# Position terms of the attention keys: added by VectorE, or by accumulating transfers onto keys that ScalarE copies

## The chip, the cores and the metric

The kernel runs on one core of one Trainium2 chip. The core has five engines with a queue each: TensorE (PE, with its weight loads PEld), VectorE (DVE), ScalarE (ACT), GpSimd (POOL) and SyncE (SP, which here only issues transfers). They work at the same time and wait for each other through semaphores. Sixteen DMA engines move data between DRAM and the on-chip memory SBUF; matrix products land in a second on-chip memory, PSUM. The metric is the device time of one execution in microseconds (us); less is better.

## What is computed

Eight images of 512 channels x 32 x 32 pass through two blocks. The change lies in the first block, in an attention over the 1024 pixels of an image. Cut to it, with `cbs` for convolution, normalization and silu:

```python
def bot_attention(x, qkv_w, rw, rh):
    b, c, h, w = x.shape
    hw = h * w
    qkv = conv2d(x, qkv_w, 0).reshape(b, 3, HEADS, HD, hw)
    q, k, v = (qkv[:, 0], qkv[:, 1], qkv[:, 2])
    r = (rw + rh).reshape(1, HEADS, HD, hw)
    logits = jnp.einsum('bhdi,bhdj->bhij', q, k + r) * HD ** (-0.5)
    a = jax.nn.softmax(logits, axis=-1)
    out = jnp.einsum('bhij,bhdj->bhdi', a, v)
    return out.reshape(b, c, h, w)
...
t = cbs(x, cv1_w, cv1_bn, 0)
ys = [t[:, :C], t[:, C:]]
for i in range(N):
    yi = ys[-1]
    z = cbs(yi, m_cv1_w[i], m_cv1_bn[i], 1)
    z = bot_attention(z, m_qkv_w[i], m_rw[i], m_rh[i])
    z = jax.nn.silu(bn_eval(conv2d(z, m_cv2_w[i], 0), m_cv2_bn[i]))
    ys.append(yi + z)
return cbs(jnp.concatenate(ys, axis=1), cv2_w, cv2_bn, 0)
```

There are 4 heads of 64 channels (so 256 channels, two halves of 128 partitions), N = 2 layers, and all is fp32. What matters is `k + r`: the position terms `r` are the same for every image. The second block (a depthwise 3x3 convolution of nine taps per channel, then a 1x1 convolution, both with a pruning of channels) is computed between the parts of the next image's attention.

## The kernel before

An image is a tile of [128 partitions, 4 chunks, 1024 pixels]. For each image, and each of the two layers, the stages are: the 3x3 convolution by a Winograd-like transform (`conv3`: products into `ps_c3`), queries, keys and values (`qkv`), attention (`attention`), a 1x1 convolution with residual (`cv2m`); then the convolution over the four parts (`last_conv` or `quartered`) and the second block.

The order of work is written out by hand. Each stage registers its pieces under a short name with `add(...)`, and strings of names (`FIRST`, `HEAD`, `TAIL`, `LAST`) say in which order the pieces are issued; `go` walks such a string. Image 0 follows `FIRST`; images 1 to 7 follow `HEAD`, then `TAIL` or, for the last, `LAST`. The wrapper `InOrder` keeps the issue order on each of PE, DVE, ACT and SP, so a name that is moved in a string moves its instruction in the queue of its engine. All of these instructions carry line 105 in the profile, that of the wrapper; POOL's carry their own lines (the prune `lp` is line 615).

The names that the change and the prediction speak of:

- `k`: four pieces of matmuls that make the keys, half 0 and half 1 (k m=2 and 3 in the code), into a PSUM tile `ps_qk` of [128, 2, 512]. Such tiles come from `ps_big`, which has two buffers and is shared with the values `ps_v`, the queries and the scores `ps_s`: a new tile waits until an old one is emptied.
- `kd`: one transfer by SP that loads `r` for both halves (1 MB) from DRAM (`r_dram`, written once in image 0 by `positions`) into the tile `kr`.
- `ka`: two additions by VectorE, `kr[:, m] = ps_qk + kr[:, m]`, which also empty the PSUM tile.
- `v`, `va`: values and their copy to SBUF by ScalarE (`vt`). `q`, `qa`: the same for queries (`qy`).
- `s`, `e`, `p`, `w`: for each of 32 steps of a layer, scores on PE from `kr` and `qy` (16 steps on half 0, then 16 on half 1), exponentials on ScalarE, their sums on VectorE, products with the values on PE.
- `t`, `l`, `lr`, `lp`: taps of the depthwise convolution (VectorE), its relu and range (ScalarE), its prune (GpSimd). `X` loads the exponential's table on ScalarE.

`kr`, `vt` and `qy` also serve as scratch of `conv3` before. In image 0 the keys take another path (`columns`, `lines`), since `r` isn't in DRAM yet.

Of the kernel before, what the change touches and what calls it, by code (L numbers as in the profile page):

```python
# [12 lines left out]
ALU = mybir.AluOpType  # L13
AX = mybir.AxisListType

P = 128
B, C, F = 8, 512, 32
# [45 lines left out]

HEAD = """
    t c*2 t b im id bm c ca iv t ip t l t*2 ib lr b t*3 c bm ca b y d y bm d ya d*2 ya d*3 y P d
    Rc R d*2 P Rc R d P ya d kd Rc R B P Rc R P B*2 Rc R E P Ez Rc B R E Ez y k*3 ya k ka t X lp
    ka t*4 v*2 l t va v*2 va t lr q*2 t*2 lp t q qa s e q qa s e p s t e w t p s e w l p s*2 w
    e*2 p w s p e s w t s w t s e*2 p lr e p w*2 h z s e p w s t w s p s e p e*2 w p s w p e w s
    t e p s w s e w e t p*2 w lp t h z s*2 e p e w s*2 n e*2 w p w s nr s p e w nr e p s e w nr
    s nr t p ns l w e p*2 w lr lp w ot h s e s w p ot s w ot s e*2 p*2 e w p s w e w s e p*2 z  # L70
    sc w nc w*2 h n nc o O nr ok Ok sc z nr*3 ns o ou oa O*2 Ou sc m Oa m sc nc m ma m ma mr ma
    ot mr ma mr o nc mr d ou Ou o O d ou Ou o d O ou*2 oa Ou*2 d Oa o O P d*2 Rc d*3 R P kd d*2
    Rc R d P Rc P R B Rc P B Rc P R B*2 Rc R ou E oa Ou R Oa o O dp E Ez*2 X k v*2 k ou oa Ou
    fr*2 Oa ka fr f*2 fr f*2 dx va k v*2 va k q*2 ka q qa q qa s e s*2 e p e w p s e p w s*2 e*2
    p*2 w s*2 e*2 w*2 s g p e w*2 s e w p s*2 h g e g p w s w z p e*2 s w e g*2 s*2 w*2 p e*2 g
    p*3 g s w*2 e p s e w h s*2 e*2 p z p w*2 s p e p s n w nr*3 w e s g e p w p s e p w*2 s nc
    e nr s ns e nc w s h s p w z w e p s e w s p e*2 p sc s w e p*2 w s sc e p w*3 h n nr*4 ns z
"""

TAIL = """  # L80
# [45 lines left out]
def fast_kernel(  # L126
# [16 lines left out]
    nc = Engines(tc)  # L143
# [12 lines left out]
    def const_tile(shape, name):  # L156
        return const.tile(shape, F32, tag=name, name=name)
# [4 lines left out]
    def big_tile(name):  # L162
        return ps_big.tile([P, 2, 512], F32, tag="big", name=name)
# [33 lines left out]
    z = const_tile([P, 2, HW], "z")  # L197

    qy = const_tile([P, 2, HW], "qy")
    kr = const_tile([P, 2, HW], "kr")  # L200
# [38 lines left out]
    r_dram = [dram.tile([P, 2, HW], F32, tag=f"r{l}", name="r") for l in range(2)]  # L239
# [15 lines left out]
    sc = const_tile([P, NBN], "sc")  # L255
# [29 lines left out]
    def flat(ps):  # L285
        return ps.rearrange("p n f -> p (n f)")
# [5 lines left out]
    def phases(ap):  # L292

        return ap.rearrange("p (r h t) -> p r h t", h=F, t=F // 4)
# [12 lines left out]
    def add(name, *pieces):  # L307
        todo.setdefault(name, []).extend(pieces)
# [104 lines left out]
    def ring_load(n=1):  # L413
        for _ in range(n):
            if not sources:
                continue
            if holds and len(sources) <= holds[0]:
                waiting[0] += 1
                continue
            src = sources.pop(0)  # L420
            t = ringp.tile([P, 2048], F32, tag="ring", name="wring")
            o = t[:, : src[1]]
            if src[1] == 1024:
                o = o.rearrange("p (k o) -> p k o", o=P)
            nc.sync.dma_start(o, src[0])
            ring.append(t)
# [463 lines left out]
    def qkv(l, by_input):  # L890


        wt, tiles, values = [], {}, {}

        def weights():
            if not wt:
                wt.append(ring.pop(0)[:, : 6 * C2].rearrange("p (k o) -> p k o", k=2))
            return wt[0]

        def products(m, k):  # L900
            w = weights()
            if m not in tiles:
                tiles[m] = big_tile("ps_qk")
            for n in range(2):
                nc.tensor.matmul(
                    tiles[m][:, n, :],
                    w[:, k, m * P : (m + 1) * P],
                    z[:, k, n * 512 : (n + 1) * 512],
                    start=(k == 0),
                    stop=(k == 1),  # L910
                )

        full = [P, 4, F, F // 4]

        def load_positions():
            nc.sync.dma_start(kr, r_dram[l])

        def add_positions(m):
            nc.vector.tensor_tensor(kr[:, m, :], flat(tiles.pop(m + 2)), kr[:, m, :], ALU.add)


        def columns(m):
            col = rw[:, l, m, :].rearrange("p (t r) -> p r t", r=4)
            nc.vector.tensor_tensor(
                phases(kr[:, m, :]),
                phases(flat(tiles.pop(m + 2))),
                col.unsqueeze(2).to_broadcast(full),
                ALU.add,
            )

        def lines(m):
            row = rh[:, l, m, :].unsqueeze(1).unsqueeze(3)
            kk = phases(kr[:, m, :])
            nc.gpsimd.tensor_tensor(kk, kk, row.to_broadcast(full), ALU.add)

        def value_products(g, js):
            w = weights()
            if g not in values:
                values[g] = ps_big.tile([P, 4, C2], F32, tag="big", name="ps_v")
            for j in js:  # L940
                jt = 4 * g + j
                for k in range(2):
                    nc.tensor.matmul(
                        values[g][:, j, :],
                        z[:, k, jt * P : (jt + 1) * P],
                        w[:, k, 2 * C2 : 3 * C2],
                        start=(k == 0),
                        stop=(k == 1),
                    )

        def value_end(g):
            nc.scalar.copy(vt[:, 4 * g : 4 * g + 4, :], values.pop(g))

        def query_end(m):
            nc.scalar.copy(qy[:, m, :], flat(tiles.pop(m)))

        order = [(k, m) for m in (2, 3) for k in range(2)]
        add("k", *[lambda m=m, k=k: products(m, k) for k, m in (sorted(order) if by_input else order)])
        if by_input:
            add("ka", *[lambda m=m: columns(m) for m in range(2)])  # L960
            add("kp", *[lambda m=m: lines(m) for m in range(2)])
        else:
            add("kd", load_positions)
            add("ka", *[lambda m=m: add_positions(m) for m in range(2)])
        add("v", *[lambda g=g, j=j: value_products(g, (j, j + 1)) for g in range(2) for j in (0, 2)])
        add("va", *[lambda g=g: value_end(g) for g in range(2)])
        add("q", *[lambda m=m, k=k: products(m, k) for m in range(2) for k in range(2)])
        todo["q"].append(lambda last=todo["q"].pop(): (last(), ring_load()))
        add("qa", *[lambda m=m: query_end(m) for m in range(2)])
# [402 lines left out]
    for b in range(B):  # L1372
# [26 lines left out]
        for l in range(2):  # L1399
            conv3(l)  # L1400
            qkv(l, first)
            attention()
            cv2m(l)
# [471 lines left out]
```

## Time and profile before

| What | Value |
|---|---|
| Runs | median 2597.78 us of 4 (2596.92 to 2601.54) |
| The profiled execution | 2596.29 us, of which the span on the core is 2594.5 us |
| Granted TensorE clock | 0.998 |
| kr<-ps_qk,kr on DVE | 28 of 1.225 us (median) |
| vt<-ps_v on ACT (a copy of the same shape from PSUM) | 32 of 1.01 us (median) |
| kr<-r issued by SP | 14 of 1 MB, 7.1 us to landing (median) |
| r<-pos issued by SP | 4 of 512 KB, 3.4 us to landing (median) |
| pt<-in_x issued by SP | 32 of 512 KB, 3.9 to 11.8 us to landing (median 9.7) |
| ht<-ht,keep on POOL (the prune) | 28 of 1.12 to 2.12 us |

The span is the time from the first to the last instruction on the core. In the lines that follow, "A <- B" behind a duration says that the engine stood idle before A until B was done. A matmul of fp32 is recorded as two, and the end of a matmul is modelled, so records of neighbours overlap a little; gaps under 0.16 us between matmuls can hide in that. Times in the timeline are counted from the start of the span.

### The profile page before, as it was taken

Reading aid. Unit: us, or ns where it says so; the run is one execution under the profiler, and the core shown is the slowest. Engines: PE = TensorE matmul, PEld = TensorE weight load, DVE = VectorE, ACT = ScalarE, POOL = GpSimd, SP = SyncE. Lnnn points to the kernel's source line nnn. Section 1 sums busy time; section 2 is a strip of 40 time slices with the busy share of each in tenths; the row PEclk is TensorE's granted clock in tenths of the full one; section 3 lists DMA queues with packets and bytes.
Section 4 is the critical chain, followed back from the end, with each engine's and each line's share of the span. In section 5 each row is a group of like instructions: output and inputs, shape, how many; then the busy total and the mean of one; then the engine's idle time right before and its main releaser. Section 6 shows DMA issues by size and latency. Waiting matters only on the chain.

```text
span 2594.5 us, 36342 instructions
## 1 busy us (share of the span) xinstructions
PE 2558.0 (99%) x14806; PEld 1291.6 (50%) x14806; DVE 2084.9 (80%) x2982; ACT 1185.8 (46%) x1523; POOL 98.0 (4%) x71
## 2 busy tenths in 40 slices
PE   8999999999999999999999999999999999999997
PEld 5454463634636346463464635545355554645443
DVE  8887589877898878887788778887788877888657
ACT  3635436353462544635445344444445444353534
POOL 1000000000000000000000000000000000000000
PEclk9999999999999999999999999999999999999999
DMA  9445230522305113060130602206121151312300
GB/s 345 158 156 202 66 122 25 188 77 73 113 27 212 53 65 122 17 248 17 65 123 17 248 17 81 107 18 246 33 98 74 60 204 33 137 36 95 112 17 34
DMA packets 81773, 268.49 MB, mean 103 GB/s; under 512 B 6848, under 2 KB 37312, under 8 KB 65600
## 3 DMA queue, kind: packets, MB, share of 16 engines
q1 hardware_dynamic: 78048, 262.69, 28.5%
q10 hardware_dynamic: 3552, 3.41, 0.4%
q8 instruction: 118, 1.93, 0.3%
q14 instruction: 55, 0.45, 0.1%
HBM read 212.34 MB, written 36.96 MB: 96 GB/s over the span
## 4 chain that ended last, share of the span: by engine, by line
PE 93%; DVE 3%; ACT 2%; DMA 1%; issue 0%; ACTq 0%; POOL 0%; SPq 0%; DVEq 0%
PE ps_av L105 17%; PE ps_s L105 16%; PE ps_c L105 13%; PE ps_cv L105 11%; PE ps_qk L105 8%; PE ps_cv2q L105 8%; PE ps_q L105 6%; PE ps_v L105 4%; PE ps_m L105 4%; PE ps_y L105 4%; PE ps_dn L105 2%; ACT qy L105 1%; DVE ht L105 1%; PE ps_pw L105 0%; DVE sum L105 0%
## 5 line engine op out<-in xcount | busy, mean ns | idle before, releaser
L105 ACT ACTIVATE e<-ps_s 128x1024 f32<-128x1024 f32 x512 | 509.7, 1023 | 287.5 <-PE ps_s L105 266.1
L105 PE MATMUL ps_s<-qy,kr 64*64 64x512 f32 x4096 | 514.6, 592 | 1.5
L105 DVE TENSOR_TENSOR sum<-sum,e 128x1024 f32<-128x1024 f32 x384 | 475.6, 1238 | 40.2 <-ACT e L105 21.0
L105 PE MATMUL ps_av<-e,vt 64*64 64x512 f32 x4096 | 507.0, 590 | 0.0
L105 DVE SCALAR_TENSOR_TENSOR ht<-xn,v_sb,ht 128x961 f32<-128x961 f32 (+1 forms) x256 | 312.3, 1228 | 8.3 <-ACT ht L105 5.0
L105 PEld LDWEIGHTS ps_s<-qy,kr 64*64 64x64 f32 x4096 | 160.8, 132 | 288.8 <-issue 183.7
L105 PEld LDWEIGHTS ps_av<-e,vt 64*64 64x64 f32 x4096 | 165.9, 133 | 277.0 <-issue 266.5
L105 PE MATMUL ps_qk<-z,wring 128*128 128x512 f32 x512 | 229.8, 596 | 2.0 <-ACT z L105 1.3
L105 DVE TENSOR_TENSOR sum<-e 128x1024 f32<-128x1024 f32 x64 | 78.2, 1221 | 126.1 <-ACT e L105 124.8
L105 ACT COPY c<-ps_c 128x256 f32<-128x256 f32 x96 | 35.6, 371 | 262.3 <-PE ps_c L105 262.3
L105 PEld LDWEIGHTS ps_qk<-z,wring 128*128 128x128 f32 x512 | 95.7, 190 | 118.5 <-issue 100.0
L105 DVE RECIPROCAL r<-ps_dn 128x128 f32<-128x128 f32 x128 | 112.8, 923 | 11.3 <-PE ps_dn L105 9.0
L105 PEld LDWEIGHTS ps_c<-kr,wring 128*128 128x128 f32 x1024 | 116.8, 192 | 8.0 <-issue 7.7
L105 PE MATMUL ps_c<-vt,wring 128*128 128x128 f32 x1024 | 118.2, 276 | 2.1 <-DMA wring<-u 1.4
L105 PE MATMUL ps_c<-qy,wring 128*128 128x128 f32 x1024 | 117.3, 275 | 0.5 <-ACT c L105 0.5
L105 PEld LDWEIGHTS ps_c<-vt,wring 128*128 128x128 f32 x1024 | 116.2, 192 | 3.0 <-ACT c L105 2.4
L105 PE MATMUL ps_c<-kr,wring 128*128 128x128 f32 x1024 | 117.0, 275 | 0.0
L105 PE MATMUL ps_cv<-pt,w_sb 128*128 128x512 f32 x256 | 116.7, 607 | 0.0
L105 PEld LDWEIGHTS ps_c<-qy,wring 128*128 128x128 f32 x1024 | 115.7, 192 | 0.7 <-ACT c L105 0.7
L105 PE MATMUL ps_v<-wring,z 128*128 128x256 f32 x512 | 114.8, 379 | 0.7 <-DVE kr L105 0.7
L105 PE MATMUL ps_m<-z,wm_sb 128*128 128x512 f32 x256 | 112.5, 592 | 0.0
L105 PE MATMUL ps_y<-pt,w_sb 128*128 128x512 f32 x256 | 112.3, 592 | 0.0
(177 smaller groups left out, 3233.2 us busy)
## 6 DMA issues: line engine op xcount, KB each, us to landing
wring<-u SPq DMA_DIRECT2D x96, 1024.0 KB, 4.9
pt<-in_x SPq DMA_DIRECT2D x32, 512.0 KB, 9.7
rw<-r SPq DMA_DIRECT2D x64, 256.0 KB, 3.4
xt<-in_x SPq DMA_DIRECT2D x32, 512.0 KB, 5.9
out<-xt SPq DMA_DIRECT2D x32, 512.0 KB, 3.3
kr<-r SPq DMA_DIRECT2D x14, 1024.0 KB, 7.1
wring<-q SPq DMA_DIRECT2D x14, 896.0 KB, 5.7
wring<-in_wqkv SPq DMA_DIRECT2D x16, 768.0 KB, 4.6
```

What stands on the lines that cost most here:

```text
L105: made = method(*args, **kwargs)
```

## The change

Keys are copied from PSUM to `kr` by ScalarE (`ka` is now that copy), and the position terms are added to them by one transfer of GpSimd for each half that accumulates from DRAM into `kr` (`kd`, now behind `ka`). The load of `r` by SP is gone. The string `HEAD` has the new names in their places and some others moved; it has two names more than before. The descriptor scratch that the program sets aside is given a size of 2048 bytes per partition, where before nothing was said of it.

```diff
-        def load_positions():
-            nc.sync.dma_start(kr, r_dram[l])
+        def keys(m):
+            nc.scalar.copy(kr[:, m, :], flat(tiles.pop(m + 2)))
 
         def add_positions(m):
-            nc.vector.tensor_tensor(kr[:, m, :], flat(tiles.pop(m + 2)), kr[:, m, :], ALU.add)
+            nc.gpsimd.dma_start(kr[:, m, :], r_dram[l][:, m], accum_op=ALU.add)
...
-            add("kd", load_positions)
-            add("ka", *[lambda m=m: add_positions(m) for m in range(2)])
+            add("ka", *[lambda m=m: keys(m) for m in range(2)])
+            add("kd", *[lambda m=m: add_positions(m) for m in range(2)])
...
-    nc = bacc.Bacc("TRN2", target_bir_lowering=False, num_devices=1)
+    nc = bacc.Bacc("TRN2", target_bir_lowering=False, num_devices=1, dynamic_dma_scratch_size=2048)
```

In `HEAD`, around the keys of the first and of the second layer:

```diff
-    Rc R d*2 P Rc R d P ya d kd Rc R B P Rc R P B*2 Rc R E P Ez Rc B R E Ez y k*3 ya k ka t X lp
-    ka t*4 v*2 l t va v*2 va t lr q*2 t*2 lp t q qa s e q qa s e p s t e w t p s e w l p s*2 w
+    Rc R d*2 P Rc R d ya P d Rc R B P Rc R P B*2 Rc R E P Ez Rc B R E Ez y k*3 ya k ka X lp ka
+    kd*2 t*5 v*2 l t va v*2 va t lr q*2 t*2 lp t q qa s q e qa s e p s t e w t s e w l s*2 p*2 w
...
-    ot mr ma mr o nc mr d ou Ou o O d ou Ou o d O ou*2 oa Ou*2 d Oa o O P d*2 Rc d*3 R P kd d*2
+    mr ot mr ma mr o nc mr ou d Ou o O d ou Ou o d O ou*2 oa Ou*2 d Oa o O P d*2 Rc d*3 R P d*2
...
-    Rc R d P Rc P R B Rc P B Rc P R B*2 Rc R ou E oa Ou R Oa o O dp E Ez*2 X k v*2 k ou oa Ou
-    fr*2 Oa ka fr f*2 fr f*2 dx va k v*2 va k q*2 ka q qa q qa s e s*2 e p e w p s e p w s*2 e*2
+    Rc R d P Rc P R B Rc P B Rc P R B*2 Rc R ou E oa Ou R Oa o O dp E Ez*2 X k v k v ou oa Ou
+    fr*2 Oa ka kd f*2 fr*2 f*2 dx va k v*2 k va q*4 ka kd qa*2 s*3 e*2 p e w p s e w s*2 e*2 p*3
```

The rest of `HEAD` has further moves by a place or a few of sums, products and checks (`p`, `w`, `ot`, `sc`, `m`, `fr`, `g`).

More of the change, by code (lines that the diff above doesn't have):

```diff
@@ L65 @@
     t c*2 t b im id bm c ca iv t ip t l t*2 ib lr b t*3 c bm ca b y d y bm d ya d*2 ya d*3 y P d
-    Rc R d*2 P Rc R d P ya d kd Rc R B P Rc R P B*2 Rc R E P Ez Rc B R E Ez y k*3 ya k ka t X lp
-    ka t*4 v*2 l t va v*2 va t lr q*2 t*2 lp t q qa s e q qa s e p s t e w t p s e w l p s*2 w
-    e*2 p w s p e s w t s w t s e*2 p lr e p w*2 h z s e p w s t w s p s e p e*2 w p s w p e w s
-    t e p s w s e w e t p*2 w lp t h z s*2 e p e w s*2 n e*2 w p w s nr s p e w nr e p s e w nr
-    s nr t p ns l w e p*2 w lr lp w ot h s e s w p ot s w ot s e*2 p*2 e w p s w e w s e p*2 z
@@ L71 @@
-    sc w nc w*2 h n nc o O nr ok Ok sc z nr*3 ns o ou oa O*2 Ou sc m Oa m sc nc m ma m ma mr ma
-    ot mr ma mr o nc mr d ou Ou o O d ou Ou o d O ou*2 oa Ou*2 d Oa o O P d*2 Rc d*3 R P kd d*2
-    Rc R d P Rc P R B Rc P B Rc P R B*2 Rc R ou E oa Ou R Oa o O dp E Ez*2 X k v*2 k ou oa Ou
-    fr*2 Oa ka fr f*2 fr f*2 dx va k v*2 va k q*2 ka q qa q qa s e s*2 e p e w p s e p w s*2 e*2
-    p*2 w s*2 e*2 w*2 s g p e w*2 s e w p s*2 h g e g p w s w z p e*2 s w e g*2 s*2 w*2 p e*2 g
-    p*3 g s w*2 e p s e w h s*2 e*2 p z p w*2 s p e p s n w nr*3 w e s g e p w p s e p w*2 s nc
@@ L77 @@
-    e nr s ns e nc w s h s p w z w e p s e w s p e*2 p sc s w e p*2 w s sc e p w*3 h n nr*4 ns z
+    Rc R d*2 P Rc R d ya P d Rc R B P Rc R P B*2 Rc R E P Ez Rc B R E Ez y k*3 ya k ka X lp ka
+    kd*2 t*5 v*2 l t va v*2 va t lr q*2 t*2 lp t q qa s q e qa s e p s t e w t s e w l s*2 p*2 w
+    e*2 p w s p e s w t s w t e s e p lr e p w*2 h z s e p w s t w s p s e p e*2 w*2 p s e w s t
+    e p s w p s e w e t p*2 w lp t h z s*2 e*2 w s*2 n e p*2 e w*2 s nr s p e w nr e p s e w nr
+    s nr t p ns l w e p*2 w lr lp w ot h s e s w p ot w s w s e*2 p*2 e w p s e w s e ot p*2 z
@@ new lines @@
+    sc w nc w*2 h n nc o O nr ok Ok z nr*2 sc nr ns o ou oa O*2 Ou sc Oa m sc nc m*2 ma*2 m ma
+    mr ot mr ma mr o nc mr ou d Ou o O d ou Ou o d O ou*2 oa Ou*2 d Oa o O P d*2 Rc d*3 R P d*2
+    Rc R d P Rc P R B Rc P B Rc P R B*2 Rc R ou E oa Ou R Oa o O dp E Ez*2 X k v k v ou oa Ou
+    fr*2 Oa ka kd f*2 fr*2 f*2 dx va k v*2 k va q*4 ka kd qa*2 s*3 e*2 p e w p s e w s*2 e*2 p*3
+    w s*2 g e*2 w*2 s p e w*2 s e w p s*2 h g e g p w s w z p e*2 s w e g*2 s*2 w*2 p e*2 g p*3
+    g s w*2 e p s e w h s*2 e*2 p z p w*2 s p e p s n nr*3 w e s g e p w p s w*3 e p s nc e nr s
@@ L78 @@
+    ns e nc w s h s p w z w e p s e w s p e*2 p sc s w e p*2 w s sc e p w*3 h n nr*4 ns z
 """
```

## The prediction

> **What bounds the kernel now.** I read the page first (busy time by engine, then the chain that ended last), then TensorE's own waits for everything after the first image, then the timelines of the two stages in which keys are made, and last the windows of DMA load around them.
>
> The page's engine shares and its chain of waits:
>
> ```profile
> PE 2558.0 (99%) x14806; PEld 1291.6 (50%) x14806; DVE 2084.9 (80%) x2982; ACT 1185.8 (46%) x1523; POOL 98.0 (4%) x71
> PE 93%; DVE 3%; ACT 2%; DMA 1%; issue 0%; ACTq 0%; POOL 0%; SPq 0%; DVEq 0%
> ```
>
> TensorE (PE) carries 93% of the chain and VectorE (DVE) 3%. A busy PE need not be a full one, so I ask how regular it is. The windows of whole stretches of 315 us (columns: us, then busy us and count of PE, PEld, DVE, ACT, POOL, then clock, DMA share, GB/s):
>
> ```profile
> 955.00:1270.00 315.00, 314.75 (x1842) 159.36 (x1841) 256.48 (x369) 143.97 (x188) 10.71 (x7) 1.00 0.27 97
> 1270.00:1585.00 315.00, 314.75 (x1842) 159.16 (x1842) 256.87 (x369) 144.00 (x187) 10.70 (x7) 1.00 0.27 97
> ```
>
> PE idles 0.25 us in 315. All that PE waited for from 320 us to the end:
>
> ```profile
> PE ps_pw L105 <- DVE wring L105: 4.7, 1, 4.7
> PE pv L105 <- DVE d L105: 1.7, 2, 0.8
> PE ps_c L105 <- ACT c L105: 0.5, 1, 0.5
> PE pv L105 <- DVE flag L105: 0.4, 1, 0.4
> PE pk L105 <- DVE gm L105: 0.3, 1, 0.3
> ```
>
> That is 7.6 us in all, and none of it names kr. The waits on kr (0.7 us) lie before 320 us, in the first image, which takes another path (`columns`/`lines`). The changed path runs 7 images x 2 layers = 14 times.
>
> Now the stage of layer 0 in the second image (start, duration, engine, what, count; a fp32 matmul is recorded as two):
>
> ```profile
> 372.30 7.03 PE L105 MATMUL ps_qk<-z,wring 128*128 128x512 f32 x16
> 375.93 1.23 DVE L105 TENSOR_TENSOR kr<-ps_qk,kr 128x1024 f32<-128x1024 f32 x1 [3.89 <-PE ps_qk L105]
> 379.16 7.07 PE L105 MATMUL ps_v<-wring,z 128*128 128x256 f32 x32
> 379.36 1.23 DVE L105 TENSOR_TENSOR kr<-ps_qk,kr 128x1024 f32<-128x1024 f32 x1 [1.02 <-PE ps_qk L105]
> 391.31 1.09 PE L105 MATMUL ps_s<-qy,kr 64*64 64x512 f32 x8
> ```
>
> The keys of half 0 are out of PSUM at 377.2, and the first score that reads them starts at 391.3: PE fills the gap with values and queries. Layer 1, the same image:
>
> ```profile
> 510.14 3.60 PE L105 MATMUL ps_qk<-z,wring 128*128 128x512 f32 x8
> 512.06 1.22 DVE L105 TENSOR_TENSOR kr<-ps_qk,kr 128x1024 f32<-128x1024 f32 x1 [0.93 <-PE ps_qk L105]
> 513.57 3.62 PE L105 MATMUL ps_v<-wring,z 128*128 128x256 f32 x16
> 525.70 3.32 PE L105 MATMUL ps_s<-qy,kr 64*64 64x512 f32 x24
> ```
>
> And the load on the DMA engines in these two stages (the share is the last column but one):
>
> ```profile
> 379.00:383.00 4.00, 4.00 (x19) 3.40 (x18) 3.60 (x4) 0.00 (x0) 0.65 (x1) 1.00 0.02 4
> 383.00:387.00 4.00, 4.00 (x18) 3.13 (x18) 3.89 (x5) 2.87 (x3) 0.00 (x0) 1.00 0.00 0
> 504.00:530.00 26.00, 25.92 (x103) 13.39 (x105) 15.29 (x19) 11.86 (x13) 0.00 (x0) 1.00 0.94 356
> ```
>
> Layer 0 has idle DMA engines, layer 1 nearly full ones: there the loads of pt and xt and the stores of out pass.
>
> **What the Trainium skill says.** "DMA: Bandwidth & Descriptors", section "SWDGE vs HWDGE vs iDMA": an accumulating transfer has to be issued by GpSimd, whose cores write its descriptors in software; the same page's "Anatomy of one DMA — SWDGE (gpsimd) path" prices a plain one at about 2.0 us plus bytes / 436e3, here 2.0 + 524,288 / 436e3 = 3.2 us, and "Latency and other measured facts" puts its first byte at about 1 us. The trace of before has no transfer from GpSimd; its plain 512 KB transfers from SP take 3.4 us (r<-pos, median) on free engines and 11.8 us at worst (pt<-in_x) in the crowd of layer 1. "SBUF — State Buffer", section "Who interferes with whom": GpSimd and VectorE share a port pair, and an instruction of one with two SBUF inputs holds up one of the other that reads SBUF. The trace agrees: the prune on POOL takes 1.12 us in the best case and 2.12 us beside taps with two SBUF inputs. It infers that descriptor writing is not held by such VectorE work, only by its two-port modes. No page prices the accumulation itself.
>
> **The change part by part.**
>
> *VectorE loses the addition.* 28 TENSOR_TENSOR kr<-ps_qk,kr of 1.225 us = 34.3 us less, so 2084.9 becomes about 2050.6. It is worth nothing to the end: in the steady images PE idles 0.25 us.
>
> *ScalarE gains a copy.* 28 copies of 128x1024 from PSUM; the same form is there as vt<-ps_v, 1.01 us. 28 x 1.01 = 28.3 us, 1185.8 becomes about 1214. In layer 0 the first stands behind y<-ps_y, which ends at 373.98, and before the table load; it runs when its matmuls end, 375.93 to 376.94. The load and the 0.20 us warm-up follow until 378.4; the second copy starts at 379.4, undelayed, and ends at 380.4. So PSUM is freed 0.2 us earlier than now, and the values that take these buffers (379.2 and 382.6) don't wait. Behind them in ScalarE's queue stand ht (waits for taps that VectorE now does about 4 us earlier, since it no longer waits for ps_qk) and vt, which still finds its matmuls ended at 382.6.
>
> In layer 1 PE's order becomes k v k v for k v v k in pieces of 1.72 us: the first key half ends at 510.1 rather than 511.9, the copy at 511.2, before PE wants the buffer at 511.8. va ends at 512.9, the values that reuse its buffer start at 513.5: 0.6 us to spare. The second key half moves to 517.0–518.7, its copy after va on ScalarE to 519.8; the second query tile needs that buffer at 522.1. Nothing stalls. The other swaps move single scores or values in PE's queue. Counted in the order of both programs, a score stays at least 2 pieces behind the score whose PSUM buffer it takes (as before) and a value 3 pieces behind its score (as before), at 0.86 us a piece against 1.02 us of exponential. Cost: 0.
>
> *SP loses the loads of kr* (14 issues, of 1 MB). In layer 1 this takes 1 MB out of the full stretch before 500 us; the ring loads behind it come earlier. Worth 0: no wait of PE after 320 us is on a DMA.
>
> *GpSimd gains 28 issues.* In layer 0 the prune stands ahead of them; its keep is computed once VectorE is through with y, near 372.2, so even 2.12 us of it ends by 374.4, before the copy. Behind the two issues stands the next prune, at 390.7 now, whose result is needed some 60 us later.
>
> *The new wait.* PE's first score of a layer waits for the accumulation of half 0, with all of attention behind it in PE's queue. Room from the end of the copy: layer 0 391.31 − 376.94 = 14.4 us; layer 1 525.70 − 511.2 = 14.5 us. Half 1 is read by the 17th score, near 418.6 in the timeline of layer 0: 38 us of room. Bounds of the time from copy to landing: below, 1 + 3.2 = 4.2 us by the page. Above, the accumulation also reads its destination: I double the trace's times, 1 + 2 x 3.4 = 7.8 us in layer 0 and 1 + 2 x 11.8 = 24.6 us in layer 1. The worst pt stands last of four in one queue behind other loads; GpSimd's has a queue of its own (so the first section named; the engines alternate between queues), so I take 8 us for layer 0 and 10 us for layer 1. Both are inside the room: cost 0.
>
> *The smaller scratch* sets how many descriptors can be outstanding. Two transfers at a time and over 100 us between pairs: I take 0. If it held up the second of a pair, that one has 38 us.
>
> Sum: 0 on PE. The profiled execution took 2596.3 us (span 2594.5 and 1.8 around it); the median of the runs is 2597.8, 1.5 us above it, and that is what I forecast. Its own range, from the spread of the runs shown and small shifts of the end, is 2594 to 2602.
>
> **Rivals.** About 0.2%, 5.2 us, is what a measurement of this kernel can tell from no change.
>
> *Late landing in layer 1 (slower).* From 14.5 us between copy and landing on, each further us costs 7 us. At 16 us: 7 x 1.5 = 10.5, so 2608; at the upper bound of 24.6 us: 7 x 10.1 = 71, so 2669. For it: the share of 0.94, the untried accumulation. Against it: its own queue and 1 MB less ahead.
>
> *GpSimd is held up by VectorE in layer 0 (slower).* The taps run back to back there until 391.8. If descriptors were written only in the gaps after that, the landing would be at about 391.8 + 4.2 = 396: 4.7 us late, 7 x 4.7 = 33, so 2631. For it: the doubled prune. Against it: the page's inference, and that writing is not reading.
>
> *VectorE's relief reaches PE (faster).* At most the 7.6 us of waits after 320 us, so 2590. Of these 4.7 us lie at the end of the last image, where the chain is VectorE's work on the last convolution, which doesn't begin earlier; against it, then, the regular 0.25 us.
>
> **How the numbers follow.** Hidden on both layers 0.66; late landing 0.19; held-up descriptors 0.08; relief 0.07. That gives within 0.2% 0.66, slower 0.27, faster 0.07. The range runs from 2592.5, the edge of no change, to 2614, which takes in late landings up to 2.3 us at one layer; left out are 0.07 below and some 0.13 above.
>
> **What would show it.** ACT near 1214 and DVE near 2051 us; a new queue of about 15 MB or its double; no wait of ps_s on kr among PE's waits; the steady windows still at 314.75 of 315. A wait of PE ps_s on the DMA kr<-r, seven or fourteen times, would prove the forecast wrong, and its length the landing time; a wait of ps_v or ps_qk on ACT kr would show the 0.6 us margin mistaken.

## The result, and the profile after

| Kernel | Median | Range | Runs |
|---|---|---|---|
| before | 2598.06 us | 2596.57 to 2601.54 | 52 |
| changed | 2595.51 us | 2593.91 to 2596.44 | 32 |

The ratio is 0.9989, its 95% interval 0.9985 to 0.9994: 2.55 us faster (1.6 to 3.9 by the interval). That is little, inside the 0.2% that the forecast set as its bound, but it is not nothing: the interval leaves 1 out, and no change had been forecast. The profiled execution of before (2596.29 us) lies below all 52 runs of before, so the two profiles, 2594.5 and 2593.9 us of span, show only part of the difference; e4_before, below, finds out why.

The page of the changed kernel (engine shares; the queues with packets, MB and share of the 16 engines; one row of the DMA issues):

```profile
PE 2557.1 (99%) x14806; PEld 1291.6 (50%) x14806; DVE 2054.8 (79%) x2954; ACT 1213.9 (47%) x1551; POOL 130.2 (5%) x99
...
q1 hardware_dynamic: 76032, 248.01, 27.2%
q0 software_dynamic: 4032, 14.68, 3.1%
...
kr<-r POOLq DMA_DIRECT2D x28, 512.0 KB, 6.6
```

VectorE has lost 30 us and ScalarE gained 28. A new queue carries 14.68 MB, counted once. All that TensorE waited for from 320 us on:

```profile
PE ps_pw L105 <- DVE wring L105: 4.7, 1, 4.7
PE pv L105 <- DVE d L105: 1.7, 2, 0.8
PE pv L105 <- DVE flag L105: 0.5, 1, 0.5
PE pk L105 <- DVE gm L105: 0.2, 1, 0.2
```

There is no wait on kr, and one line of before is gone, PE ps_c <- ACT c. Windows of the same two stretches read as before; they cannot show the gain, because a stretch of fixed length is full of records either way:

```profile
955.00:1270.00 315.00, 314.79 (x1842) 159.50 (x1841) 252.56 (x366) 148.22 (x192) 15.16 (x11) 1.00 0.29 97
1270.00:1585.00 315.00, 314.78 (x1841) 159.38 (x1840) 251.41 (x364) 147.77 (x192) 16.25 (x11) 1.00 0.29 97
```

The timeline of layer 0 in the second image, keys to first score:

```profile
376.58 1.01 ACT L105 COPY kr<-ps_qk 128x1024 f32<-128x1024 f32 x1 [1.95 <-PE ps_qk L105]
...
378.17 1.05 POOL L919 DMA_DIRECT2D kr<-r  x1 [3.30 <-ACT kr L105]
...
381.55 0.87 POOL L919 DMA_DIRECT2D kr<-r  x1 [2.33 <-issue]
...
391.96 1.09 PE L105 MATMUL ps_s<-qy,kr 64*64 64x512 f32 x8
```

From the ps_qk of this layer (372.95) to the first score it takes 19.01 us, as before (391.31 − 372.30). Layer 1:

```profile
510.77 1.01 ACT L105 COPY kr<-ps_qk 128x1024 f32<-128x1024 f32 x1 [1.29 <-PE ps_qk L105]
...
512.08 0.89 POOL L919 DMA_DIRECT2D kr<-r  x1 [70.42 <-ACT kr L105]
...
512.50 1.01 ACT L105 COPY vt<-ps_v 128x1024 f32<-128x1024 f32 x1 [0.71 <-PE ps_v L105]
...
514.01 3.62 PE L105 MATMUL ps_v<-wring,z 128*128 128x256 f32 x16
...
526.14 2.26 PE L105 MATMUL ps_s<-qy,kr 64*64 64x512 f32 x16
```

From the ps_qk of layer 1 to its first score it takes 20.83 us in both (505.31 to 526.14, and 504.87 to 525.70 before). The stages in which keys are made cost what they cost before. So the gain lies elsewhere. Aligning the starts of TensorE's work in both traces, one place differs in nearly every image: the sums of the exponentials at the end of layer 0's attention. VectorE collects them in the tile `sum`, and TensorE adds them over the partitions by a product with ones, into `ps_dn`. Its weight load for the second half of ps_dn waits there for VectorE's sum. Two images of before, then two of after (start, duration; in brackets the wait of the weight load):

```profile
1400.75 0.14 PEld L105 LDWEIGHTS ps_dn<-sum,ones 128*32 128x32 f32 x4 [0.69 <-DVE sum L105]
1717.19 0.14 PEld L105 LDWEIGHTS ps_dn<-sum,ones 128*32 128x32 f32 x4 [0.69 <-DVE sum L105]
```

```profile
1716.60 0.14 PEld L105 LDWEIGHTS ps_dn<-sum,ones 128*32 128x32 f32 x4 [0.50 <-DVE sum L105]
2032.83 0.14 PEld L105 LDWEIGHTS ps_dn<-sum,ones 128*32 128x32 f32 x4 [0.50 <-DVE sum L105]
```

The image takes 316.44 us before and 316.23 after. The wait is 0.69 or 0.70 us in all seven images of before, and 0.49 or 0.50 in six of the changed kernel. In its fifth image it is 0.85 us. VectorE was some 0.2 us late there already, and then GpSimd's prune takes 3.11 us and VectorE stands idle for it inside the chain that ends in the sum:

```profile
1388.55 3.11 POOL L615 TENSOR_SCALAR ht<-ht,keep 128x1024 f32<-128x1024 f32 x1 [12.76 <-DVE keep L105]
...
1391.70 1.23 DVE L105 TENSOR_TENSOR pt<-ht,pt 128x1024 f32<-128x1024 f32 x1 [0.94 <-POOL ht L615]
```

In the next image the same prune takes 2.02 us, and VectorE doesn't wait for it. TensorE's own row hides the wait for the sum, since the eight matmuls are merely recorded as a longer group. Before:

```profile
1399.92 1.89 PE L105 MATMUL ps_dn<-sum,ones 128*32 128x512 f32 x8
```

After:

```profile
1715.96 1.69 PE L105 MATMUL ps_dn<-sum,ones 128*32 128x512 f32 x8
```

### The profile page after: what moved, and what is told of

Same layout as the page of the kernel before. It is cut to its first block, busy times and chain, and to the rows that moved or that the text cites. A ratio compares the mean times of both kernels' runs of the same rounds, so it can differ in the third digit from the quotient of the medians.

```text
span 2593.9 us, 36377 instructions
## 1 busy us (share of the span) xinstructions
PE 2557.1 (99%) x14806; PEld 1291.6 (50%) x14806; DVE 2054.8 (79%) x2954; ACT 1213.9 (47%) x1551; POOL 130.2 (5%) x99
## 3 DMA queue, kind: packets, MB, share of 16 engines
q1 hardware_dynamic: 76032, 248.01, 27.2%
q0 software_dynamic: 4032, 14.68, 3.1%
## 4 chain that ended last, share of the span: by engine, by line
PE 94%; DVE 3%; ACT 1%; issue 1%; DMA 0%; ACTq 0%; POOL 0%; SPq 0%; DVEq 0%
PE ps_av L105 16%; PE ps_s L105 16%; PE ps_c L105 13%; PE ps_cv L105 11%; PE ps_qk L105 8%; PE ps_cv2q L105 8%; PE ps_q L105 7%; PE ps_v L105 4%; PE ps_m L105 4%; PE ps_y L105 4%; PE ps_dn L105 1%; ACT qy L105 1%; DVE sum L105 1%; DVE ht L105 1%; PE ps_pw L105 0%
## 5 line engine op out<-in xcount | busy, mean ns | idle before, releaser
L105 DVE SCALAR_TENSOR_TENSOR ht<-xn,v_sb,ht 128x961 f32<-128x961 f32 (+1 forms) x256 | 317.5, 1248 | 8.6 <-ACT ht L105 5.0
```

What stands on the lines that cost most here:

```text
L105: made = method(*args, **kwargs)
```

## The experiments

Each was run beside the kernel before; the medians of before were 2597.98 to 2598.75 us. The changed kernel's 2595.51 us is from its own runs above. Most ratios lie within 0.5% of 1, so an interval that holds 1 settles nothing by time; there the traces are compared. The theories of where the gain comes from: ORDER (other moves in HEAD), RELIEF (VectorE's time saved reaches TensorE), SCRATCH (the smaller descriptor scratch), CHANCE (the scatter of the runs), and, formed after the first four runs, TAIL (the order of VectorE's sums at the end of layer 0's attention) and SP-LOAD (the load that SP no longer issues).

### Order and keys apart

e1_order: the order of the changed kernel with the keys of before.

```diff
-    Rc R d*2 P Rc R d P ya d kd Rc R B ...
+    Rc R d*2 P Rc R d ya P d kd Rc R B ...
...
-    ... Ez*2 X k v*2 k ou oa Ou
+    ... Ez*2 X k v k v ou oa Ou
```

> The arithmetic of the kernel before (SP loads the position terms, VectorE adds them, kd and ka at their old places among their neighbours), every other name in HEAD where the changed kernel has it. Theory ORDER (the swaps of other names bring the gain): about 2595.5 us, ratio about 0.999. Theory RELIEF (VectorE's 2.45 us less per layer reach TensorE): 2598 us, no gain, and the second weight load of ps_dn at the end of layer 0's attention waits 0.70 us for the sum as before.

Measured: 2602.99 us, ratio 1.0019 (1.0012 to 1.0027). Slower, which neither theory had. In its timeline two new waits stand, one in each layer:

```profile
386.30 1.98 PE L105 MATMUL ps_qk<-z,wring 128*128 128x512 f32 x4 [0.25 <-ACT vt L105]
...
512.43 1.98 PE L105 MATMUL ps_qk<-z,wring 128*128 128x512 f32 x4 [0.31 <-DVE kr L105]
```

In layer 1 the order k v k v wants the PSUM buffer of the first keys back earlier, and VectorE, which has two reductions ahead of the addition, empties it late. In layer 0 both additions now stand ahead of VectorE's taps, which end later, so ScalarE's ht and the copy of the values behind it come later too (384.11 against 383.04, 385.25 against 384.19). The image takes 317.31 us. But ps_dn's wait is 0.49 or 0.50 us here: that part comes with the order.

e2_mech: the reverse, the keys of the changed kernel in the order of before (shown against before; the two `kd` of SP are gone too).

```diff
-    ... k*3 ya k ka t X lp
-    ka t*4 v*2 l t va
+    ... k*3 ya k ka t X lp
+    ka kd*2 t*4 v*2 l t va
...
-    fr*2 Oa ka fr f*2 fr f*2 dx va k v*2 va k q*2 ka q qa
+    fr*2 Oa ka kd fr f*2 fr f*2 dx va k v*2 va k q*2 ka kd q qa
```

> The new keys (ScalarE's copy, GpSimd's accumulating transfer, scratch of 2048) in the old order of HEAD; only kd is moved to stand behind ka. Theory RELIEF: about 2595.5 us, and the wait of ps_dn's second weight load on the sum is 0.50 us, not 0.70. Theory ORDER: 2598 us.

Measured: 2607.05 us, ratio 1.0035 (1.0023 to 1.0047), 9 us slower, and ps_dn waits 0.69 us. The place is layer 1 alone:

```profile
511.97 1.01 ACT L105 COPY kr<-ps_qk 128x1024 f32<-128x1024 f32 x1 [3.02 <-PE ps_qk L105]
...
513.03 1.98 PE L105 MATMUL ps_qk<-z,wring 128*128 128x512 f32 x4 [1.10 <-ACT kr L105]
```

With k v v k the keys' copy stands ahead of the values' copy in ScalarE's queue and waits for keys that end late; behind it vt starts at 512.88, where before it had started at 510.34. TensorE then finds neither buffer free. The image takes 317.80 us, so the loss is about 7 x 1.36 us. So k v k v is what ScalarE's copies need, and what VectorE's additions can't use. Neither half, as cut here, is faster alone.

### The scratch, and the scatter of the runs

e3_scratch:

```diff
-    nc = bacc.Bacc("TRN2", target_bir_lowering=False, num_devices=1, dynamic_dma_scratch_size=2048)
+    nc = bacc.Bacc("TRN2", target_bir_lowering=False, num_devices=1)
```

> The changed kernel without the smaller scratch. Theory SCRATCH (the gain comes from it): 2598 us. RELIEF and ORDER: as the changed kernel, about 2595.5 us.

Measured: 2594.70 us, ratio 0.9988 (0.9981 to 0.9994). The scratch's size is worth nothing that shows.

e4_before has no edit.

> The kernel before once more, unchanged: how far two sets of runs of the same program differ, and a second profile of it. Theory CHANCE (the gain is the scatter of runs and of the first image): its median lies 1 us or more from 2598 us and its ratio's interval leaves 1 out. All others: 2598 us within 0.5, ratio 1.000.

Measured: 2597.84 us, ratio 0.9999 (0.9991 to 1.0007). CHANCE falls. Its trace has a wait that the first profile of before had only in small, and under another name:

```profile
1448.93 0.79 PE L105 MATMUL ps_c<-qy,wring 128*128 128x128 f32 x5 [1.02 <-DMA wring<-u]
```

This ring load (weights of conv3 in layer 1) is issued by SP at 1440.70, right behind kr<-r. The tile's own view, of this execution of before and of the changed kernel at the same point of the image:

```profile
L105 SPq DMA_DIRECT2D wring<-u x1: 319/319/319, 1440.7 to 1440.7; - x1
...
DMA to landing us min/median/max: 8.1/8.1/8.1
```

```profile
L105 SPq DMA_DIRECT2D wring<-u x1: 320/320/320, 1440.0 to 1440.0; - x1
...
DMA to landing us min/median/max: 4.8/4.8/4.8
```

TensorE wants it some 7.2 us after its issue (1440.70 to 1447.9). In the seven images it lands after 6.1 to 7.6 us in the first profile of before and 6.0 to 8.1 us in this one; in the changed kernel after 4.6 to 5.2. In the first profile the 7.6 us are in the third image, where TensorE's wait of 0.52 us was put down to ACT c, done long before. So the load that SP lost had stood ahead of a transfer that TensorE now and then waited for.

More than half of the difference between the two profiles of before is something else. TensorE's last 32 matmuls, in the first profile:

```profile
2568.48 15.49 PE L105 MATMUL ps_pw<-ht,wring 128*128 128x512 f32 x32 [4.75 <-DVE wring L105]
```

In this one, then in the changed kernel:

```profile
2569.58 16.93 PE L105 MATMUL ps_pw<-ht,wring 128*128 128x512 f32 x32 [4.74 <-DVE wring L105]
```

```profile
2567.02 16.20 PE L105 MATMUL ps_pw<-ht,wring 128*128 128x512 f32 x32 [4.75 <-DVE wring L105]
```

The granted clock (the last column but two) of a window there, in the first profile of before and in this one:

```profile
2568.00:2576.00 8.00, 7.52 (x14) 3.41 (x15) 5.31 (x6) 2.48 (x3) 0.00 (x0) 0.79 0.00 0
```

```profile
2568.00:2576.00 8.00, 6.42 (x8) 2.71 (x9) 6.25 (x7) 1.54 (x2) 0.00 (x0) 0.57 0.00 0
```

The clock is at half for 3.4 us in the first profile, and for 6.8 us in this one and in the changed kernel's, from within the wait ahead of these matmuls on. Of the 2.6 us between the two spans of before (2594.5 and 2597.1), the last matmuls make 1.4 and the waits of ps_c 0.9 (1.02 and 0.38 here, 0.52 there). The gain of the change is not the clock's: among runs with a mean clock of 0.998 the medians are 2597.47 us (58 runs of before, taken beside the experiments) and 2594.90 (12 of the changed kernel), with 0.997 they are 2598.49 (61) and 2595.72 (22).

### Tail, new keys without it, SP's load and VectorE's load

e5_tail: in the kernel before, one line of HEAD.

```diff
-    s nr t p ns l w e p*2 w lr lp w ot h s e s w p ot s w ot s e*2 p*2 e w p s w e w s e p*2 z
+    s nr t p ns l w e p*2 w lr lp w ot h s e s w p ot w s w s e*2 p*2 e w p s e w s e ot p*2 z
```

> The kernel before with one swap of HEAD alone, at the end of layer 0's attention: one ot (an addition of VectorE that doesn't depend on the sums) moves from before the last five sums to between the third and the fourth of them, and two w go ahead of an s. Theory TAIL (this swap is most of the gain, because two sums of the same tile back to back take 1.33 us from start to start and a sum beside an ot 1.14): 7 x 0.2 = 1.4 us less, 2596.6 us, and ps_dn's wait on the sum 0.50 us. Theory RELIEF or SP-LOAD (the rest of the change brings the gain): 2598 us.

Measured: 2595.79 us, ratio 0.9993 (0.9985 to 1.0002). The median is 2.3 us lower, more than was expected, but the interval holds 1, so the time alone doesn't show it. The trace does: ps_dn waits 0.49 to 0.50 us in all seven images, which take 316.22 us where nothing else happens. VectorE's chain at the end of layer 0 of the last image, before:

```profile
2341.29 1.21 DVE L105 TENSOR_TENSOR pt<-ht,pt 128x1024 f32<-128x1024 f32 x1
2342.43 1.21 DVE L105 TENSOR_TENSOR pt<-ht 128x1024 f32<-128x1024 f32 x1
2343.56 6.53 DVE L105 TENSOR_TENSOR sum<-sum,e 128x1024 f32<-128x1024 f32 x5
2350.01 0.69 DVE L105 TENSOR_TENSOR z<-ps_av,part 128x512 f32<-128x512 f32 x1
```

After:

```profile
2341.55 3.87 DVE L105 TENSOR_TENSOR sum<-sum,e 128x1024 f32<-128x1024 f32 x3
2345.33 1.22 DVE L105 TENSOR_TENSOR pt<-ht 128x1024 f32<-128x1024 f32 x1
2346.47 2.55 DVE L105 TENSOR_TENSOR sum<-sum,e 128x1024 f32<-128x1024 f32 x2
2348.93 0.68 DVE L105 TENSOR_TENSOR z<-ps_av,part 128x512 f32<-128x512 f32 x1
```

Work it from the starts. Five sums take 6.45 us (2343.56 to 2350.01), two take 2.46 (2346.47 to 2348.93): each further sum directly behind one of the same tile takes 1.33. An ot takes 1.14 to the next start. The same work, with one pair of dependent sums split by an ot that depends on neither, is 0.19 us shorter. The chain has no gap in either kernel (the changed kernel's fifth image apart), so TensorE gets these 0.19 us.

e6_kvkv: e2_mech with k v k v in layer 1 (shown against e2_mech); the tail stays as before.

```diff
-    ... X k v*2 k ou oa Ou fr*2 Oa ka kd fr f*2 fr f*2 dx va k v*2 va k q*2 ka kd q qa q qa
+    ... X k v k v ou oa Ou fr*2 Oa ka kd f*2 fr*2 f*2 dx va k v*2 k va q*4 ka kd qa*2
```

> The new keys in the old order, but with the changed kernel's order of keys and values (k v k v) in layer 1. The stall of 1.10 us per image of PE ps_qk on ACT kr should be gone under every theory. TAIL: 2598 us, as before, with 0.69 us of wait at ps_dn. RELIEF or SP-LOAD: about 2595.5 us.

Measured: 2596.21 us, ratio 0.9995 (0.9986 to 1.0003). The stall is gone, ps_dn waits 0.69 us again in six images of seven (1.04 in one), and the image takes 316.43 us as before. What it gains beside the kernel before (1.9 us by the medians, with 1 inside the interval) can't be the tail; its ring loads in layer 1 land after 4.7 to 5.2 us.

e7_load: the changed kernel with SP's load put back.

```diff
+            add("kx", lambda: nc.sync.dma_start(kr, r_dram[l]))
...
-    Rc R d*2 P Rc R d ya P d Rc R B ...
+    Rc R d*2 P Rc R d ya P d kx Rc R B ...
...
-    ... P d*2 Rc d*3 R P d*2
+    ... P d*2 Rc d*3 R P kx d*2
```

> The changed kernel with the old 1 MB load of the position terms by SP put back at its old places (ScalarE's copy overwrites what it brings). SP-LOAD (the gain is the shorter queue of SP, whose ring loads come earlier): about 2598 us or at least 1 us more than the changed kernel. TAIL and RELIEF: 2595.5 us.

Measured: 2595.77 us, ratio 0.9992 (0.9984 to 1.0000). The effect foreseen was not there in that size: 0.26 us over the changed kernel, less than the 0.8 us by which the medians of that kernel and its twin without the scratch differ. At equal clock it is 0.3 to 0.6 us over the changed kernel (2595.23 against 2594.90 with 0.998, 2596.29 against 2595.72 with 0.997). In the trace the mechanism is there: the ring loads land after 5.9 to 7.6 us again, and ps_c waits twice, 0.6 us in all. The view puts these waits down to DVE sd, but the ring loads land at 498.0 and 814.6, and the matmuls start at 498.2 and 814.8. A load that lies near its limit costs only in those images in which it lands over it.

e8_dve: VectorE's load put back on it.

```diff
+            add("kx", *[lambda m=m: nc.vector.tensor_tensor(qy[:, m, :], qy[:, m, :], qy[:, m, :], ALU.add) for m in range(2)])
...
-    ... ka ...
+    ... ka kx ...
```

> The changed kernel with an addition of 128x1024 on VectorE put back behind each key copy (of queries' old bytes onto themselves, overwritten later), 28 in all, some 34 us of VectorE. RELIEF (VectorE's time saved is what TensorE gains): 2598 us or more. TAIL and SP-LOAD: 2595.5 us, up to 2599 if the addition delays the values' copies in layer 0 as the keys on VectorE did in the first experiment (0.25 us of PE ps_qk on ACT vt).

Measured: 2595.16 us, ratio 0.9988 (0.9981 to 0.9995). The page of this run:

```profile
PE 2555.4 (99%) x14806; PEld 1292.8 (50%) x14806; DVE 2085.9 (80%) x2982; ACT 1213.8 (47%) x1551; POOL 136.5 (5%) x99
```

VectorE is as busy as before the change (2084.9), and the kernel as fast as the changed one. RELIEF is worth nothing that shows.

### Using what was found, and two prices

e9_ot: the changed kernel with the third ot taken out of the tail.

```diff
-    ... w s w s e*2 p*2 e w p s e w s e ot p*2 z
+    ... w s w s e*2 p*2 e w p s e w s e p*2 z
...
-    mr ot mr ma mr o nc mr ou d Ou ...
+    ot mr ot mr ma mr o nc mr ou d Ou ...
```

> The changed kernel with the third ot of layer 0 (t3, first needed some 20 us later) moved out of VectorE's chain at the end of the attention, to just ahead of the first mr, where VectorE idles 1.89 us waiting for m. Theory TAIL (VectorE's chain of sums is what TensorE waits for there, so that taking 1.14 us out of it frees TensorE until the last exponential limits, 2347.01 + 1.22 in the last image): the second ps_dn load's wait 0.50 falls to about 0.28 us, 7 x 0.22 = 1.5 us less, 2594.0 us. If the chain is not the limit: 2595.5 us.

Measured: 2590.87 us, ratio 0.9969 (0.9957 to 0.9981): 4.6 us under the changed kernel, three times what was expected. VectorE now waits for the last exponential, and TensorE for nothing; first VectorE's last sum, then the matmuls of ps_dn in another image:

```profile
2342.88 1.23 DVE L105 TENSOR_TENSOR sum<-sum,e 128x1024 f32<-128x1024 f32 x1 [0.30 <-ACT e L105]
```

```profile
1713.04 1.06 PE L105 MATMUL ps_dn<-sum,ones 128*32 128x512 f32 x8
```

The group shrinks from 1.69 to 1.06 us: with both sums ready, the second wait goes whole and not only by 0.22 us. The image takes 315.61 us, 0.62 less.

e12_d: as e9_ot, and

```diff
-    ot mr ot mr ma mr o nc mr ou d Ou ...
+    ot mr ot mr ma d mr o nc mr ou Ou ...
```

> As e9_ot, and the first d of layer 1 (1.28 us of VectorE) moved from behind the first ou, where VectorE runs without a gap for 16 us up to ps_c<-vt, to ahead of the third mr, into a gap of 1.0 us. If VectorE's chain there is what takes back TensorE's 0.35 us at ps_c<-vt (0.21 us of wait in the changed kernel): 0.33 us an image less beyond e9_ot, 2591.7 us. If not: as e9_ot, or 0.3 us an image more, by which the third mr is late.

Measured: 2588.06 us, ratio 0.9960 (0.9946 to 0.9973). In this order d reads yp before the last two residual additions reach it, so layer 1's first transform runs partly on old values: it says what 1.28 us taken out of VectorE's gapless stretch would be worth, about 2.8 us over e9_ot, but it is no way to get it.

e10_twice:

```diff
-            nc.gpsimd.dma_start(kr[:, m, :], r_dram[l][:, m], accum_op=ALU.add)
+            for _ in range(2):
+                nc.gpsimd.dma_start(kr[:, m, :], r_dram[l][:, m], accum_op=ALU.add)
```

> The changed kernel with each accumulating transfer issued twice (so the position terms are added twice; the output differs for that reason). It prices a late landing. From the profile of the changed kernel: copy end to issue 0.6 us, issue to landing 6 to 10.5 us; a second one that starts after the first lands at about 14 us in layer 0 and 14 to 20 us in layer 1, against the room of 14.4 us. If the room is as worked out: 2595.5 us if the two overlap, 7 x 0 to 6 us more, up to 2638 us, if they run one after the other, with PE ps_s waiting for the DMA kr<-r. If GpSimd's issues were held up by VectorE: tens of us more.

Measured: 2631.79 us, ratio 1.0131 (1.0116 to 1.0147). Layer 1, where the copy ends at 510.86 in this run:

```profile
528.78 4.22 PE L105 MATMUL ps_s<-qy,kr 64*64 64x512 f32 x24 [3.49 <-DMA kr<-r]
```

GpSimd issues the second only when the first has landed (511.16 and 519.94). The two take 17.9 us from the copy, against the room of 14.4: TensorE waits the difference. In layer 0 it doesn't wait for half 0. GpSimd was not held up. Six such waits make 24.6 us of the 32.0 by which this profile's span, 2626.0 us, exceeds the changed kernel's. The granted clock takes the rest, as far as the trace shows: it goes to half before or at the end of each of the six waits, for 3.4 us in four images and 6.8 in two. A window at the first:

```profile
528.00:532.00 4.00, 3.22 (x20) 0.99 (x24) 0.00 (x0) 1.02 (x1) 0.00 (x0) 0.57 1.04 306
```

So a us of waiting costs about 1.3 us here. The room was judged right, and a single transfer, which in the changed kernel lands 5.7 to 9.8 us after an issue 0.3 to 0.6 us behind the copy, leaves some 4 us of it in the worst case.

e11_load3:

```diff
-            add("kx", lambda: nc.sync.dma_start(kr, r_dram[l]))
+            add("kx", lambda: [nc.sync.dma_start(kr, r_dram[l]) for _ in range(3)])
```

> The changed kernel with the old 1 MB load by SP put back three times at each of its old places. Theory SP-LOAD (part of the gain: without the load, the ring loads wring<-u behind it in SP's queue come earlier, and ps_c's occasional wait on them goes): in layer 1 the ring loads come up to 5.9 us later than with one load (2 MB at the 356 GB/s of that stage), ps_c waits for wring<-u in every image, 2600 to 2640 us. If SP's loads don't matter: 2595.5 us.

Measured: 2676.07 us, ratio 1.0293 (1.0279 to 1.0307): dearer than expected, because the three write one tile and SP's queue waits for one before it issues the next (10.7 us for kr<-r in this stretch). SP's issues in layer 1:

```profile
487.47 0.33 SPq L105 DMA_DIRECT2D wring<-u  x1
487.96 11.87 SPq L105 DMA_DIRECT2D kr<-r  x3
499.92 0.65 SPq L105 DMA_DIRECT2D wring<-u  x1
```

TensorE waits for wring<-u 64.7 us in seven times, of the 81 us by which the span is longer; the granted clock, 0.984 in the mean and at half for 10.2 us from within each wait on, goes with the rest. It shows that what stands behind this load is the ring load TensorE needs next; its size is that of a blocked queue, not of bandwidth.

### Without the new keys

e13_kdlate: the kernel before, SP's load in layer 1 behind two more ring loads.

```diff
-    ... P d*2 Rc d*3 R P kd d*2
-    Rc R d P Rc P R B ...
+    ... P d*2 Rc d*3 R P d*2
+    Rc R d P Rc P kd R B ...
```

> The kernel before (keys added by VectorE) with its load of the position terms in layer 1 moved two ring loads later in SP's queue, still some 17 us ahead of its use. SP-LOAD: the ring load that followed it lands 4.7 to 5.2 us after its issue as in the changed kernel, not 6.0 to 8.1, ps_c's wait of up to 1.0 us past 320 us is gone, and the median falls by 0.5 to 1.2 us, to 2597.2 us, with a narrower range. If the old keys or chance make up the rest of the gain: 2598 us.

Measured: 2597.14 us, ratio 0.9995 (0.9987 to 1.0004). The ring load lands after 4.7 to 4.9 us in five images, 5.9 and 6.5 in two; ps_c waits for nothing past 320 us. The median moved as foreseen, but the interval holds 1: the mechanism is shown, its worth only bounded. The range, 2596.03 to 2599.45 us, is hardly narrower. The profiled execution is one of the longest (2599.25 us) and says why: its first image, which the change doesn't touch, waits 3.5 us for a ring load (1.4 in before's profile) and then has 3.4 us at half clock, so that the second image's keys start at 375.50 rather than 372.30.

e14_oldkeys: as e13_kdlate, with the tail of the changed kernel and e9_ot's move.

```diff
-    ... lp w ot h s e s w p ot s w ot s e*2 p*2 e w p s w e w s e p*2 z
+    ... lp w ot h s e s w p ot w s w s e*2 p*2 e w p s e w s e p*2 z
...
-    ... m ma m ma mr ma ot mr ma mr o
+    ... m ma m ma ot mr ma ot mr ma mr o
```

> As e13_kdlate, with the order at the end of layer 0's attention (ot, w) as in the changed kernel and the third ot moved out to ahead of the first mr as in e9_ot: old keys, three moves of order. If the gains are of order and of SP's queue and need no new keys: about what e9_ot took, 2591 us. If VectorE's relief is needed for them: 2593.5 us or more.

Measured: 2590.85 us, ratio 0.9973 (0.9963 to 0.9984), the same as e9_ot, with the keys added by VectorE as ever; the image takes 315.63 us. Of the versions that compute all of the reference, these two are the fastest.

## Why the prediction was wrong by a little

*The sum.* "Sum: 0 on PE" failed in two of its terms. "The other swaps move single scores or values in PE's queue ... Cost: 0" looked at TensorE's queue only. One swap moved an ot in VectorE's queue, where a gapless chain ends in what TensorE waits for: 0.2 us an image, 1.5 us in seven by the image times of e5_tail, of which the changed kernel's fifth image takes back 0.35. And of SP's load, "Worth 0: no wait of PE after 320 us is on a DMA": the profile of before had its one such wait, 0.5 us, under ScalarE's name. In the profiles that have SP's load once at or near its old places, before, e1_order, e4_before, e5_tail and e7_load, ps_c waits 0.5 to 1.4 us past 320 us; in the changed kernel, e2_mech, e3_scratch, e6_kvkv and e9_ot not at all (0.3 us in e8_dve). A third, small part is left open: in the last image the profiles with VectorE's keys (before, e1_order, e4_before, e5_tail, e13_kdlate, e14_oldkeys) lose 0.35 us between the keys of layer 0 and those of layer 1 (132.92 us against 132.57 in the image ahead of it in before; 132.35 in both in the changed kernel), and the cause was not followed. Together, with 0.5 to 1.4 us for SP's load, that makes 2.0 to 2.9 us, against 2.55 measured. The first part is shown by the traces, and e9_ot and e14_oldkeys show by their times that this chain is what TensorE waits for. The second is shown by its mechanism, and its size (e7_load 0.26, e13_kdlate 1.1 us) lies within the scatter.

*VectorE's addition is worth nothing to the end*: right (e8_dve), though "PE idles 0.25 us" was no proof of it. The wait of ps_dn's weight load didn't show as idle time of TensorE but as a longer group of matmuls. *The rival "VectorE's relief reaches PE"* had the right sign and bounded it by visible waits; what came was not the relief but the order of VectorE's chain, and a shorter queue of SP.

*ScalarE's copy*: 28 x 1.012 us, 1213.9 against 1214. VectorE 2054.8 against 2050.6: it lost the 34 us and took 4 back, while its taps grew by 5 (317.5 us in all, against 312.3); why they grew was not followed.

*k v k v for k v v k, "Nothing stalls"*: right, with 0.5 us between the end of va (513.51) and the values (514.01) for the 0.6 foreseen. The prediction took the swap for harmless; it was needed, at 1.36 us an image (e2_mech).

*The landing*: from the end of the copy 8 us were taken for layer 0 and 10 for layer 1; it was 6.0 to 7.0 and 7.2 to 10.2. The lower bound of 4.2 us was the Trainium skill's price ("DMA: Bandwidth & Descriptors", "Anatomy of one DMA — SWDGE (gpsimd) path") plus 1 us for the first byte. The page's fixed 2.0 us already hold set-up and completion, so that us is counted twice; as a bound it held. The price of a late landing was too low: the wait came out as worked, 3.5 us where two transfers outran the room by 3.5, but with the lower clock a us of it cost about 1.3 (e10_twice). *Held-up descriptors*: didn't happen; issues take 0.85 to 1.06 us beside back-to-back taps, as the Trainium skill infers ("SBUF — State Buffer", "Who interferes with whom"). *The smaller scratch at 0*: right (e3_scratch).

*The base.* The forecast took the median of four runs and no change. The step to it, "1.5 us above" the profiled execution, was itself a sign, not followed, that this profile is a fast one of its kernel: beside the next profile of before it has less of the ring load's waits (0.9 us) and 3.4 us less at half clock near its end (1.4 us).

## What to carry to other kernels

When an engine is "99% busy", its waits are hidden in stretched groups: compare the time from one image to the next, and the length of a group of equal work, before a wait is called absent. When an order is changed, follow each moved name in the queue of its own engine and ask whether that queue ends in something the bound engine waits for; here the move that gave most was on VectorE, and neither it nor SP's shorter queue needed a new way of adding. And one profile of a kernel whose runs scatter upwards shows the good case: a second one would have shown the transfer that lands near its limit, and that the same matmuls at the end of the run take 15.5 or 16.9 us, as the granted clock is.

## What the runs showed of the hardware, unexpected

- Two VectorE additions of 128x1024 in which the second reads what the first wrote start 1.33 us apart; with an independent one between, each starts 1.14 us after its forerunner. The Trainium skill ("VectorE: DVE Perf Modes", "The DRAIN you can't avoid") has it that a semaphore behind each of eight copies cost nothing extra. That can't be carried over to these additions: a dependence costs 0.19 us here.
- An accumulating transfer of 512 KB from GpSimd lands 5.7 to 6.5 us after its issue in layer 0, where the DMA engines do little else, and 6.8 to 9.8 us in layer 1, where they are nearly full. Plain transfers of that size by SP took 3.4 us (r<-pos, from SBUF to DRAM) and 4.2 us (wring<-in_w, from DRAM to SBUF; medians of before). The 14.68 MB of the 28 are counted once, but per MB they kept the DMA engines busy about twice as long as the transfers of the large queue: 3.1% of the span for 14.68 MB, against 27.2% for 248.01.
- A transfer's landing moves with what stands ahead of it in the queue: 1 MB ahead of the ring load, issued about 3 us earlier (1437.55 and 1440.70), adds 1.2 to 3.3 us to the 4.8 us that it takes without.
- Where TensorE waited 3.5 us or more after the first image (e10_twice, e11_load3, and 4.7 us near the end of every profile), the granted clock went to half within the wait or at most 0.3 us after it, for 3.4, 6.8 or 10.2 us. Around waits of up to 1.1 us (ps_c, and ps_qk in e2_mech) it stayed full.
